# More products of constants at the front, and copies of probabilities ahead of exponentials in the fourth and the last four units

## The chip, the cores and the metric

The kernel runs on one core of one Trainium2 chip. The metric is device time in microseconds (us) of one execution. Three runs of the kernel before took 1654.76, 1656.32 and 1657.05 us; their median, 1656.32 us, is the time before.

A core has five engines that run side by side, each through its own list of instructions in order: PE (TensorE, matrix products; PEld are its weight loads), DVE (VectorE), ACT (ScalarE), POOL (GpSimd) and SP (SyncE, which here only issues transfers). An instruction waits at the head of its engine's list until what it reads is there and what it overwrites has been read; all that stands behind it on that engine waits too. SP's list of transfers obeys the same rule: a transfer whose source isn't ready holds up the transfers behind it.

## The reference, cut to what matters

The input x has 32 sequences of 100 tokens with 512 features, the context 32 sequences of which the first 100 tokens matter under the causal mask. A cross-attention with 16 heads of 32 features is added to x, and then a feed-forward part, a shared expert for all tokens plus 16 experts that each take 12 tokens of every sequence:

```python
q = (Q @ WQ.T).reshape(B, Sq, NHEAD, D_K).transpose(0, 2, 1, 3)
k = (K @ WK.T).reshape(B, Skv, NHEAD, D_K).transpose(0, 2, 1, 3)
v = (V @ WV.T).reshape(B, Skv, NHEAD, D_K).transpose(0, 2, 1, 3)
scores = jnp.einsum('bhqd,bhkd->bhqk', q, k) / jnp.sqrt(jnp.float32(D_K))
scores = jnp.where(causal, scores, -jnp.inf)
attn = jax.nn.softmax(scores, axis=-1)
y = jnp.einsum('bhqk,bhkd->bhqd', attn, v)
...
x = x + y @ Wfc.T + bfc                      # Q is layernorm(x), K and V the context
x = x + experts(layernorm(x)) + shared(layernorm(x))
```

## The kernel before

Large products are made of two halves: each operand is split into a rounded part and the rest, `split` (L103) with a copy on ACT and a subtraction on DVE, and `mm3` (L49, its products are line L56) sums three products per piece. A group of one output tile is therefore 12 products.

**Units.** The attention works in `NU` = 32 units. Unit u is four sequences (`sb`) and one group of four heads (`c`): u = 4 sb + c. Counting from 0, the fourth unit is u = 3, the last four are u = 28 to 31. The steps of a unit are spread over three rounds of the loop (L576), a software pipeline whose order is written out by hand for PE, ACT, DVE, SP and POOL: in round u the kernel makes the queries of unit u (`qproj`, `qkeep`), the softmax of unit a = u - 1, and the values of unit back = u - 2. For one unit the steps are:

- `scores`: 16 products into a PSUM tile sc, of which there is one.
- `sm_max` (DVE, L278) and `sm_sub` (POOL, L287) for each half (hb = 0, 1: two sequences each); `sm_exp` (ACT, L293, two instructions for a half); `sm_sum` (DVE, L298 and L299) and `sm_mul` (POOL, L304) for each half.
- `p_turn(u, b)` for b = 0 to 3: four transposes of probabilities on PE (L310) into a PSUM tile ms, of which there are two, used in turn; `p_keep(u, b)`: the copy of these on ACT (L315), which empties the bank.
- `values`: 16 products (L325) into the next ms tile; `y_keep`: a split of y (L104, L105) and its store to DRAM (yD, issued by SP at L335).

Between these steps stand the projections of the context's keys and values: `kproj`/`kkeep` (a copy on ACT at L226 and a store kD<-kk that SP issues at L232), `vproj`/`vkeep` (L206, L208). `kload` (L237) and `vload` (L242, one load of 800 KB for four units) read them back. PSUM tiles kv, of which there are two, hold the projections in turn.

In a round the copies of b = 0, 1 follow `sm_exp(a, 0)`, and those of b = 2, 3 follow `sm_exp(a, 1)` and the key projection. Round u = 2 alone has all four turns and copies ahead of both exponentials.

**The front.** `prologue` (L340) begins with `WARM` = 8 products of a tile of constants by itself (L345); their result isn't used, and they need no load. Then come the loads and splits of WK, the first context block, WV and the second block, and the groups kproj(0, 0..3), vproj(0, 0..1), kproj(1, 0..3).

**The end of the attention.** Unit 28 is the last round of the loop; in it the last block's `kproj(8, 3)` stands between the turns of b = 0, 1 and of b = 2, 3, and `kkeep` behind all copies. `vload` for the last four units stands ahead of that `kkeep`, and so its transfer ahead of the transfer kD<-kk. Then `pr.load_y()` (L704) loads yh and yl (L1099), the attention's result of the first 384 tokens, and `last_units` (L431) writes out the rounds 29 to 31 together with the first steps of the feed-forward part, in `pr` (class `Prep`): `fc(i)` (12 products of yh, yl with Wfc into a kv tile), `add` (DVE, L1119, reads that tile), `bias` (POOL, L1110), `stats`, `rsqrt`, `norm` (DVE, L1140), `turn` (transposes on PE at L1050, copy at L1051, rest at L1052). After them the gate and up products of the shared expert start (tile gu), and the rest of the kernel, from about 360 us on, is the feed-forward part, which the diff doesn't touch.

Of the kernel before, what the change touches and what calls it, by code (L numbers as in the profile page):

```python
# [29 lines left out]
BUF = dict(cr=4, raw=6, cx=8, x=2, xr=3, v=2, kk=2, kt=2, vt=2, q=3, p=5, pt=5, y=2, pj=2, sc=1, tr=2)  # L30
GROUPS = [3, 2, 3, 3, 3, 3, 3, 3, 2]
GMAX = 384
WARM = 8
NSLOT = B * CAP
NST = NSLOT // 128
EPS = 1e-5
# [24 lines left out]
def attention(tc, K, F):  # L61
    nc = tc.nc
    with ExitStack() as ctx, ExitStack() as kvctx:
# [57 lines left out]
        def split_wc(w, c, r, eng=None):  # L121
            cs = slice(c * 128, (c + 1) * 128)
            split(WH[w][:, :, cs], WL[w][:, :, cs], r.rearrange("p (d n) -> p d n", d=NC4), eng)
# [122 lines left out]
        def qproj(u):  # L246
            sb, c = divmod(u, NC4)
            cs = slice(c * 128, (c + 1) * 128)
            nh, nl = cur["xh", sb], cur["xl", sb]
            pq = ps_kv.tile([128, D], F32, name="kv")  # L250
            mm3(nc, pq[:, 0:SB], [((WH[2][:, d, cs], WL[2][:, d, cs]),
                                   (nh[:, d, :], nl[:, d, :])) for d in range(NC4)])
            return pq

        def qkeep(u, pq):
            q = qp.tile([128, SB], F32, name="q")
            nc.scalar.copy(q, pq[:, 0:SB])
            cur["q", u] = q

        def scores(u):  # L260
            q, kt = cur["q", u], cur["k", u]
            sc = ps_sc.tile([S, 4, D], F32, name="sc")
            for b in range(4):
                cs = slice(b * S, (b + 1) * S)
                for h in range(4):
                    rows = slice(32 * h, 32 * h + 32)
                    nc.tensor.matmul(sc[:, h, cs], q[rows, cs], kt[rows, cs], start=True, stop=True)  # L267
            cur["sc", u] = sc
# [20 lines left out]
        def sm_exp(u, hb):  # L289
            p = cur["p", u, hb][0]  # L290
            for bb in range(2):
                b = u // NC4 * 4 + hb * 2 + bb
                nc.scalar.activation(p[:, bb], p[:, bb], AF.Exp, scale=rstd[:, b:b + 1])  # L293
# [8 lines left out]
        def sm_mul(u, hb):  # L302
            pv, sm = cur["p", u, hb][1], cur["sm", u, hb]
            nc.gpsimd.tensor_tensor(pv, pv, sm[:, :, None].to_broadcast([S, 8, S]), ALU.mult)  # L304
# [8 lines left out]
        def p_keep(u, b):  # L313
            pt = ptp.tile([128, 4, S], F32, name="pt")[0:S]
            nc.scalar.copy(pt, cur["tp", u, b][0:S, :, 0:S])  # L315
            cur["pt", u, b] = pt
# [20 lines left out]
        NU = nsb * NC4  # L337
# [78 lines left out]
        def turns(u, *bs):  # L416
            for b in bs:
                p_turn(u, b)

        def keeps(u, *bs):  # L420
            for b in bs:
                p_keep(u, b)
# [8 lines left out]
        def last_units(pr):  # L431

            gp, mt = nc.gpsimd, pr.pt

            def kt_bank():
                return ps_kv.tile([128, D], F32, name="kv").rearrange("p (c t) -> p c t", c=NC4)

            def maxes(u):
                for hb in range(2):
                    sm_max(u, hb)  # L440
                    sm_sub(u, hb)

            u = NU - 3
            kload(u)
            for i in range(pr.nt):
                pr.load_x(i)
            kload(u + 1)
            sm_max(u - 1, 0)
            sm_sub(u - 1, 0)
            y_keep(u - 3)  # L450
            sm_max(u - 1, 1)
            sm_sub(u - 1, 1)
            qkeep(u, qproj(u))
            turns(u - 2, 0, 1)
            keeps(u - 2, 0, 1)
            turns(u - 2, 2, 3)
            sm_exp(u - 1, 0)
            keeps(u - 2, 2, 3)
            sm_exp(u - 1, 1)
            for hb in range(2):  # L460
                sm_sum(u - 1, hb)
                sm_mul(u - 1, hb)
            pr.fc(0)
            F.chunk_load()
            values(u - 2)

            u = NU - 2
            scores(u - 1)
            y_keep(u - 3)
            pr.add(0)  # L470
            pr.bias(0)
            maxes(u - 1)
            pr.bias(1)
            pr.stats(0)
            pr.rsqrt(0)
            qkeep(u, qproj(u))
            turns(u - 2, 0, 1)
            keeps(u - 2, 0, 1)
            sm_exp(u - 1, 0)
            sm_exp(u - 1, 1)  # L480
            pr.fc(1)
            pr.norm(0)
            for hb in range(2):
                sm_sum(u - 1, hb)
                sm_mul(u - 1, hb)
            turns(u - 2, 2, 3)
            keeps(u - 2, 2, 3)
            pr.add(1)
            kload(u + 1)
            F.chunk_load()  # L490
            pr.store(0)
            pr.bias(2)
            values(u - 2)

            u = NU - 1
            scores(u - 1)
            y_keep(u - 3)
            maxes(u - 1)
            pr.fc(2)
            pr.add(2)  # L500
            pr.stats(1)
            pr.rsqrt(1)
            pr.stats(2)
            pr.rsqrt(2)
            F.ask(1, lambda: ps_kv.tile([128, D], F32, name="kv"))
            F.preps[1].load_x(0)
            F.preps[1].load_x(1)
            turns(u - 2, 0, 1)
            keeps(u - 2, 0, 1)
            qkeep(u, qproj(u))  # L510
            pr.pt = kt_bank
            pr.turn(0)
            pr.pt = mt
            pr.norm(1)
            pr.store(1)
            turns(u - 2, 2, 3)
            keeps(u - 2, 2, 3)
            pr.norm(2)
            pr.store(2)
            sm_exp(u - 1, 0)  # L520
            values(u - 2)
            sm_sum(u - 1, 0)
            sm_mul(u - 1, 0)
            y_keep(u - 2)
            pr.turn(1)
            sm_exp(u - 1, 1)
            sm_sum(u - 1, 1)
            sm_mul(u - 1, 1)
            F.chunk_cast(0, 0)

            scores(u)
            F.chunk_low(0, 0, gp)
            F.preps[1].fc(0)
            maxes(u)
            turns(u - 1, 0, 1)
            keeps(u - 1, 0, 1)
            turns(u - 1, 2, 3)
            keeps(u - 1, 2, 3)
            F.preps[1].fc(1)
            F.chunk_cast(0, 1)  # L540
            sm_exp(u, 0)
            sm_sum(u, 0)
            sm_mul(u, 0)
            pr.turn(2)
            sm_exp(u, 1)
            F.chunk_low(0, 1, gp)
            values(u - 1)
            sm_sum(u, 1)
            sm_mul(u, 1)
            y_keep(u - 1)  # L550
            F.chunk_cast(0, 2)
            scctx.close()
            F.open_gu()
            F.begin(pr.done())
            F.chunk_low(0, 2, gp)
            F.preps[1].add(0)
            F.preps[1].add(1)
            for i in range(3):
                F.chunk_cast(1, i)
                F.chunk_low(1, i, gp)  # L560
            F.preps[1].bias(0)
            F.preps[1].bias(1)
            turns(u, 0, 1)
            keeps(u, 0, 1)
            pr.logits()
            turns(u, 2, 3)
            keeps(u, 2, 3)
            F.begun()
            values(u)
            pr.tokens()  # L570
            y_keep(u)

        with tc.manual_schedule(engines={mybir.EngineType.Pool}):
            wq = prologue()
            ahead = False
            for u in range(NU - 3):  # L576
                sb, c = divmod(u, NC4)
                a, back = u - 1, u - 2
                a = a if a >= 0 else None
# [3 lines left out]
                kv = j in blocks  # L583
# [47 lines left out]
                if u == 1:  # L631
# [1 line left out]
                    wq_keep(2, wq[2])  # L633
                    sm_sum(a, 0)
                    sm_mul(a, 0)
                if a is not None and u > 2:
                    sm_exp(a, 0)
                if back is not None:
                    p_turn(back, 0)
                    p_turn(back, 1)  # L640
                    p_keep(back, 0)
                    p_keep(back, 1)
                if u == 2:
                    p_turn(back, 2)
                    p_turn(back, 3)
                    p_keep(back, 2)
                    p_keep(back, 3)
                    split_wc(2, 3, wq[3])
                    xt_split(1, 0)
                    sm_exp(a, 0)  # L650
                if xn:
                    x_stats(*xn)
                    if xn[1] == 3:
                        x_rstd(xn[0])
                if a is not None and u > 1:
                    sm_exp(a, 1)
                    sm_sum(a, 0)
                    sm_mul(a, 0)
                pk = kproj(j, ck) if kv else None
                if kv and vv:  # L660
                    kkeep(j, ck, pk)
                if u == 1:
# [2 lines left out]
                    sm_mul(a, 1)  # L665
                if c == 1 and u > 1 or u == NU - 4:
                    vload(sb)
                if back is not None and u > 2:
                    p_turn(back, 2)
                    p_turn(back, 3)  # L670
                    p_keep(back, 2)
                    p_keep(back, 3)
                if u == 1:
                    vkeep(j, ck, vproj(j, ck))
                    wq_less(3, wq[3])
                if kv and not vv:
                    kkeep(j, ck, pk)
                if a is not None and u > 1:
                    sm_sum(a, 1)
# [733 lines left out]
```

## Time and profile before

| what | value |
|---|---|
| median of three runs | 1656.32 us (1654.76 to 1657.05) |
| the profiled execution | 1656.77 us, its span 1655.0 us |
| PE busy, 0 to 15 us | 13.41 of 15.00 us |
| PE busy, 15 to 60 us | 44.23 of 45.00 us |
| PE busy, 60 to 75 us | 13.11 of 15.00 us |
| PE busy, 75 to 310 us | 234.25 of 235.00 us |
| PE busy, 310 to 360 us | 46.00 of 50.00 us |
| PE busy, 360 to 1655 us | 1291.29 of 1295.00 us |
| share of the chain that ended last | PE 95%, DVE 1%, POOL 1%, DMA 1%, ACT 1% |

The times are of one profiled execution; the span goes from its first to its last instruction, and the 1.77 us between span and time lie around it. Busy time of PE is modelled from the starts of pipelined products, so a busy PE can still be slow: where products of one shape follow each other, the distance of their starts tells the pace. The rows of the timeline show start, duration, engine, line, operation, the tiles written and read, the shape and a count; brackets tell how long the engine was idle before and what ended that.

The fourth unit's round lies at about 56 to 68 us, the rounds 28 to 31 at about 303 to 350 us.

### The profile page before, as it was taken

What the parts mean: (1) busy time and instruction counts of PE and PEld (TensorE: products, weight loads), DVE (VectorE), ACT (ScalarE), POOL (GpSimd) and SP (SyncE); (2) the same over time, 40 slices, a digit from 0 to 9 for tenths busy, and PEclk for the clock granted to TensorE, in tenths of its full rate; (3) what the DMA queues carried; (4) which work ended last, traced back from release to release, by engine and by line L of the source; (5) the groups of instructions that cost most, each with busy time, mean ns of one, the idle gap of its engine ahead of it and who ended that gap; (6) DMA issues with size and microseconds to landing.
All of it is one profiled execution on the core that took longest, in us unless ns stands there. A gap on an engine that the chain in (4) does not pass through costs nothing.

```text
span 1655.0 us, 27948 instructions
## 1 busy us (share of the span) xinstructions
PE 1642.3 (99%) x10722; PEld 1506.0 (91%) x10722; DVE 913.1 (55%) x2178; ACT 697.4 (42%) x1152; POOL 623.9 (38%) x501
## 2 busy tenths in 40 slices
PE   9999999999999999999999999999999999999999
PEld 8888888889899998999999999999999999999998
DVE  6878777665433434344655555555555555555542
ACT  4666666553111211123444444444444444444442
POOL 2778777660111011010743334433344443344001
PEclk9999999999999999999999999999999999999999
DMA  8566665645231223211545555455555455555452
GB/s 258 169 198 200 202 195 173 211 153 185 90 108 49 88 88 111 81 62 30 191 161 159 150 164 170 144 162 150 159 169 161 148 152 161 162 163 160 138 160 62
DMA packets 113493, 243.81 MB, mean 147 GB/s; under 512 B 16609, under 2 KB 64834, under 8 KB 113360
## 3 DMA queue, kind: packets, MB, share of 16 engines
q1 hardware_dynamic: 99856, 216.34, 39.8%
q0 software_dynamic: 13088, 25.22, 8.0%
q8 instruction: 84, 1.38, 0.3%
q14 instruction: 49, 0.40, 0.1%
q10 hardware_dynamic: 416, 0.48, 0.1%
HBM read 188.25 MB, written 53.73 MB: 146 GB/s over the span
## 4 chain that ended last, share of the span: by engine, by line
PE 95%; DVE 1%; POOL 1%; DMA 1%; ACT 1%; issue 1%; SPq 0%; POOLq 0%; ACTq 0%
PE gu L56 49%; PE dn L56 25%; PE kv L56 11%; PE m L56 3%; PE ms L310 2%; PE ms L325 1%; PE sc L267 1%; POOL p L287 1%; DMA yD<-y 0%; DVE p L278 0%; DMA yh<-yD 0%; PE m L1194 0%; DMA raw<-wA 0%; ACT pt L315 0%; POOL p L304 0%
## 5 line engine op out<-in xcount | busy, mean ns | idle before, releaser
L56 PE MATMUL gu<-xh,whl 128*128 128x384 f32 (+1 forms) x3200 | 641.2, 332 | 0.0
L56 PEld LDWEIGHTS gu<-xh,whl 128*128 128x128 f32 x3200 | 555.8, 188 | 20.3 <-issue 1.2
L1018 POOL DMA_INDIRECT gx<-xnD,iq x192 | 245.2, 1277 | 395.6 <-DVE big L1061 296.3
L56 PE MATMUL dn<-whl,hh 128*128 128x512 f32 x1168 | 366.3, 395 | 0.0
L821 DVE TENSOR_TENSOR whl<-wraw,whl 128x1536 fp32r<-128x1536 f32 x142 | 249.7, 1759 | 197.8 <-ACT whl L820 178.6
L56 PE MATMUL gu<-xl,whl 128*128 128x384 f32 (+1 forms) x1600 | 335.9, 331 | 0.0
L56 PEld LDWEIGHTS gu<-xl,whl 128*128 128x128 f32 x1600 | 279.1, 188 | 0.2 <-DVE xl L1052 0.2
L855 ACT CAST hh<-g 128x384 fp32r<-128x384 f32 (+1 forms) x200 | 101.0, 505 | 409.8 <-DVE g L852 379.2
L56 PEld LDWEIGHTS dn<-whl,hh 128*128 128x128 f32 x1168 | 215.7, 188 | 35.7
L852 DVE TENSOR_TENSOR g<-g,gu 128x384 f32<-128x384 f32 (+1 forms) x200 | 108.3, 541 | 251.0 <-PE gu L56 245.1
L820 ACT CAST whl<-wraw 128x1536 fp32r<-128x1536 f32 x142 | 209.8, 1477 | 57.2 <-PE dn L56 53.4
L56 PE MATMUL dn<-whl,hl 128*128 128x512 f32 x584 | 230.5, 395 | 0.0
L851 ACT ACTIVATE g<-gu 128x384 f32<-128x384 f32 (+1 forms) x200 | 96.2, 481 | 229.4 <-PE gu L56 229.4
L856 DVE TENSOR_TENSOR hl<-g,hh 128x384 fp32r<-128x384 f32 (+1 forms) x200 | 111.8, 559 | 114.3 <-ACT hh L855 113.8
L1073 POOL DMA_INDIRECT out_dram<-x,isl x48 | 77.7, 1619 | 171.0 <-ACT x L1072 161.2
L56 PEld LDWEIGHTS dn<-whl,hl 128*128 128x128 f32 x584 | 109.5, 188 | 26.1
L287 POOL TENSOR_TENSOR p<-p,mx 100x800 f32<-100x800 f32 x64 | 103.7, 1636 | 35.9 <-DVE mx L278 33.3
L304 POOL TENSOR_TENSOR p<-p,sm 100x800 f32<-100x800 f32 x64 | 97.4, 1528 | 35.6 <-DVE sm L299 26.2
L278 DVE CUSTOM_DVE_ANT_0 p<-sc,mask 100x100 f32<-100x100 f32 x512 | 95.5, 255 | 0.5 <-PE sc L267 0.5
L1110 POOL TENSOR_TENSOR x<-x,bfc 128x512 f32<-128x512 f32 x23 | 30.4, 1345 | 155.6 <-DMA x<-x 154.0
L293 ACT ACTIVATE p<-p,rstd 100x400 f32<-100x400 f32 x128 | 73.6, 624 | 17.6 <-POOL p L287 16.9
L1062 ACT CAST xh<-big 128x512 fp32r<-128x512 f32 x59 | 36.6, 621 | 101.4 <-DVE big L1061 101.4
(158 smaller groups left out, 1581.2 us busy)
## 6 DMA issues: line engine op xcount, KB each, us to landing
wraw<-wE SPq DMA_DIRECT2D x144, 768.0 KB
yD<-y SPq DMA_DIRECT2D x31, 400.0 KB
xr<-xT SPq DMA_DIRECT2D x32, 200.0 KB
vD<-vt SPq DMA_DIRECT2D x25, 256.0 KB
v<-vD SPq DMA_DIRECT2D x8, 800.0 KB
xnD<-xn SPq DMA_DIRECT2D x25, 256.0 KB
out_dram<-x SPq DMA_DIRECT2D x25, 256.0 KB
kt<-kD SPq DMA_DIRECT2D x31, 200.0 KB
```

The lines of the kernel that those rows point to most:

```text
L56: r = nc.tensor.matmul(out, t[0][a], t[1][b], start=(first and i == 0), stop=(last and i == n - 1))
L278: nc.vector.tensor_tensor_reduce(out=p[:, bb, h, :], in0=sc[:, h, cs], in1=mask, scale=ISCALE, scalar=NEG, op0=ALU.add, op1=ALU.max, accum ...
L287: nc.gpsimd.tensor_tensor(pv, pv, mx[:, :, None].to_broadcast([S, 8, S]), ALU.subtract)
L304: nc.gpsimd.tensor_tensor(pv, pv, sm[:, :, None].to_broadcast([S, 8, S]), ALU.mult)
L820: nc.scalar.copy(h, r)
L821: nc.vector.tensor_tensor(l, r, f32(h), ALU.subtract)
L851: nc.scalar.activation(g[:, 0:t], pg[:, 0:t], AF.Gelu)
L852: nc.vector.tensor_tensor(g[:, 0:t], g[:, 0:t], pu[:, 0:t], ALU.mult)
L855: nc.scalar.copy(hh[:, 0:t], g[:, 0:t])
L856: nc.vector.tensor_tensor(hl[:, 0:t], g[:, 0:t], f32(hh[:, 0:t]), ALU.subtract)
L1018: nc.gpsimd.indirect_dma_start(out=g[:, k, :], out_offset=None, in_=self.K.xn.rearrange("t (a f) -> (t a) f", f=128), in_offset=bass.Indir ...
L1073: ins = nc.gpsimd.indirect_dma_start(out=self.K.out, out_offset=bass.IndirectOffsetOnAxis(ap=r.isl[:, i:i + 1], axis=0), in_=o, in_offset= ...
```

## The change

It has four parts.

- `WARM` is 11 instead of 8.
- Round u = 3 gets the order of u = 2: turns and copies of b = 2, 3 directly after those of b = 0, 1, then `sm_exp(a, 0)`, `sm_exp(a, 1)`, and then the key projection.
- Round u = 28: `kproj`, the turns and copies of b = 2, 3 and `kkeep` come ahead of `sm_exp(a, 1)`. On PE the order stays; on ACT the copies and the copy kk pass two exponentials; on SP the transfer kD<-kk now stands ahead of the transfer v<-vD of `vload`.
- `last_units`: in round 29 `fc(0)` comes between the two pairs of turns, followed on ACT by `sm_exp(u - 1, 0)`, the copies of b = 2, 3 and `sm_exp(u - 1, 1)`; in round 30 the turns and copies of b = 2, 3 come between the exponentials' halves, behind `fc(1)`; in round 31 the turns and copies of b = 2, 3 come ahead of `pr.turn(0)`, and `scores(u)` and the second half of the softmax ahead of `pr.turn(1)`.

No instruction is added but the three products of constants, and none is taken away.

```diff
-WARM = 8
+WARM = 11
...
             turns(u - 2, 0, 1)
             keeps(u - 2, 0, 1)
+            pr.fc(0)
+            sm_exp(u - 1, 0)
             turns(u - 2, 2, 3)
-            sm_exp(u - 1, 0)
             keeps(u - 2, 2, 3)
             sm_exp(u - 1, 1)
...
-            pr.fc(0)
             F.chunk_load()
...
             sm_exp(u - 1, 0)
+            pr.fc(1)
+            turns(u - 2, 2, 3)
+            keeps(u - 2, 2, 3)
             sm_exp(u - 1, 1)
-            pr.fc(1)
             pr.norm(0)
...
-            turns(u - 2, 2, 3)
-            keeps(u - 2, 2, 3)
             pr.add(1)
...
             qkeep(u, qproj(u))
+            turns(u - 2, 2, 3)
+            keeps(u - 2, 2, 3)
             pr.pt = kt_bank
             pr.turn(0)
             pr.pt = mt
             pr.norm(1)
             pr.store(1)
-            turns(u - 2, 2, 3)
-            keeps(u - 2, 2, 3)
...
             y_keep(u - 2)
-            pr.turn(1)
+            scores(u)
             sm_exp(u - 1, 1)
             sm_sum(u - 1, 1)
             sm_mul(u - 1, 1)
+            pr.turn(1)
             F.chunk_cast(0, 0)
 
-            scores(u)
...
-                if a is not None and u > 2:
+                if a is not None and u > 3:
                     sm_exp(a, 0)
...
-                if u == 2:
+                early = u in (2, 3)
+                if early:
                     p_turn(back, 2)
                     p_turn(back, 3)
                     p_keep(back, 2)
                     p_keep(back, 3)
+                if u == 2:
                     split_wc(2, 3, wq[3])
                     xt_split(1, 0)
+                if early:
                     sm_exp(a, 0)
...
+                pk = None
+                if u == NU - 4:
+                    pk = kproj(j, ck)
+                    p_turn(back, 2)
+                    p_turn(back, 3)
+                    p_keep(back, 2)
+                    p_keep(back, 3)
+                    kkeep(j, ck, pk)
                 if a is not None and u > 1:
                     sm_exp(a, 1)
                     sm_sum(a, 0)
                     sm_mul(a, 0)
-                pk = kproj(j, ck) if kv else None
+                if kv and not pk:
+                    pk = kproj(j, ck)
...
-                if back is not None and u > 2:
+                if back is not None and not early and u < NU - 4:
                     p_turn(back, 2)
...
-                if kv and not vv:
+                if kv and not vv and u < NU - 4:
                     kkeep(j, ck, pk)
```

## The prediction

> **What bounds the kernel now.** I read the page first, then the PE timeline of the three places that the change touches, then what ACT and SP do there, then the DMA rates by stretch.
>
> ```profile
> span 1655.0 us, 27948 instructions
> PE 1642.3 (99%) x10722; PEld 1506.0 (91%) x10722; DVE 913.1 (55%) x2178; ACT 697.4 (42%) x1152; POOL 623.9 (38%) x501
> PEclk9999999999999999999999999999999999999999
> ```
>
> PE is the chain: only a pause of PE, or products that run slowly, can give time back. The timeline (start, length, engine, line, operation) shows both at the front:
>
> ```profile
> 1.08 3.78 PE L345 MATMUL ms<-avg 128*128 128x128 f32 x16 [1.08 <-DVE avg L342]
> 4.90 0.58 PE L56 MATMUL kv<-cxh,wh 128*128 128x256 f32 x1
> 5.66 0.58 PE L56 MATMUL kv<-cxl,wh 128*128 128x256 f32 x1 [0.17 <-DVE cxl L139]
> ...
> 9.39 0.58 PE L56 MATMUL kv<-cxh,wl 128*128 128x256 f32 x1
> ...
> 13.61 0.41 PE L56 MATMUL kv<-cxh,wh 128*128 128x256 f32 x1
> 13.83 0.41 PE L56 MATMUL kv<-cxl,wh 128*128 128x256 f32 x1
> ...
> 14.55 0.28 PE L56 MATMUL kv<-cxh,wh 128*128 128x256 f32 x1
> 14.67 0.28 PE L56 MATMUL kv<-cxl,wh 128*128 128x256 f32 x1
> ```
>
> Read the distances of starts, not lengths: equal products stand 0.213 us apart up to 14.04 and 0.118 us after (the page's PEclk line is flat and does not show it). The slow pace ends after an unbroken run of 4.65 us (9.39 to 14.04); the constants' run of 3.78 us did not end it, and pauses follow it.
>
> In the fourth unit (u = 3) PE pauses for the copies of probabilities (L315), which stand behind an exponential on ACT:
>
> ```profile
> 63.23 0.86 PE L310 MATMUL ms<-ident,p 100*100 100x100 f32 x8 [1.83 <-POOL rstd L161]
> 61.56 1.15 ACT L293 ACTIVATE p<-p,rstd 100x400 f32<-100x400 f32 x2 [2.46 <-POOL p L287]
> 62.61 0.86 ACT L315 COPY pt<-ms 100x400 f32<-100x400 f32 x2
> ```
>
> The releaser that the row names is not it: the turns need the bank of tile ms that the first L315 copy empties. In the last units:
>
> ```profile
> 314.75 0.86 PE L310 MATMUL ms<-ident,p 100*100 100x100 f32 x8 [0.39 <-ACT pt L315]
> 316.43 1.19 PE L56 MATMUL kv<-wfh,yh 128*128 128x512 f32 x4 [0.81 <-DMA yh<-yD]
> 328.82 0.89 PE L325 MATMUL ms<-pt,v 100*32 100x100 f32 x32 [0.80 <-ACT pt L315]
> 304.55 0.31 SPq L242 DMA_DIRECT2D v<-vD  x1
> 311.14 0.32 SPq L232 DMA_DIRECT2D kD<-kk  x1
> 311.52 0.43 SPq L1099 DMA_DIRECT2D yh<-yD  x1
> 306.00:311.00 5.00, 5.00 (x88) 4.53 (x90) 2.87 (x13) 4.49 (x10) 3.80 (x3) 1.00 0.55 164
> 316.00:327.00 11.00, 10.57 (x108) 8.66 (x109) 7.25 (x40) 4.79 (x11) 7.44 (x6) 1.00 1.05 382
> ```
>
> Two waits are for L315 copies, one for the load of yh. The last two rows end in DMA share and GB/s.
>
> **The front.** Three more products cost 3 x 3.78 / 8 = 1.42 us: PE reaches the first real product at 1.08 + 11 x 0.4725 = 6.28 instead of 4.90. Nothing is lost by it: twelve products at 0.213 end at 8.84, the next group starts at 8.67 now, and its third product waits for wl until 9.39 in either case (without that cover they would cost up to 1.4). What is gained is that PE runs unbroken from 1.08 (by 6.28 all but the last slice of cxl is split, and that one, ready at 7.36, is used at about 8.2). A run longer than 3.78 and at most 4.65 us ends the slow pace: between 4.9 and 5.7, at any rate before 9.39. Then kproj(0,1), its third product at 9.39, ends at 9.39 + 10 x 0.118 = 10.57, kproj(0,2) and (0,3) take 12 x 0.118 = 1.41 each, to 13.39, where vproj(0,0) starts at 15.63 now. Two vproj of 12 x 0.2275 = 2.73 reach 18.85. Here it catches: kproj(1,0) needs the bank that the vt copy empties, ACT does that behind two xnh casts, and these wait for xr ("0.28 <-DMA xr<-xT", 17.71); vt ends at 19.30. The xr issues are paced by SP (one every 0.5 us from 9.37 to 14) and the DMA share there is 0.97 to 1.03, so they do not come sooner. kproj(1,0) starts at 19.35 instead of 21.10: **-1.75 us**, bounds -2.2 (as far as vproj) and +0.2 (pace not changed). Later data has slack: values(0) has more than 4 us after the load of v.
>
> **The fourth unit.** All four turns stand together, the copies ahead of the exponential, as in u = 2, where the second pair waited 0.54 us (48.19 to 48.73). PE goes on with 0.54 instead of 2.00 us of pause: -1.46. But the next unit's scores need DVE and POOL: exp(2,0) still waits for POOL until 61.5, exp(2,1) moves only from 63.37 to 63.08 (POOL ends 63.04), so sum(2,1) comes 0.8 earlier, two L105 rows of 2.39 in all follow, then the maxes, POOL's subtraction and the copies: turns(2,2,3), at 73.83, come at 73.08. **-0.75**, bounds -1.46 and 0.
>
> **The last four units.** In u = 28 the diff places kkeep ahead of exp(27,1), and so ahead of vload, which it also passes on SP. SP takes its issues in turn. kk now follows the copies 2, 3: kproj ends at 308.67, the first copy 0.60 later (as 344.40 to 345.00), kk 0.76 behind (309.86 to 310.62): 310.03, and kD<-kk is issued 0.52 after that, at 310.55. v<-vD, issued at 304.55 before, now waits behind it until 310.93; yh and yl come at 311.3 and 311.8 with 800 KB ahead of them. v took all of 306 to 311 (164 GB/s x 5 us = 820 KB) and some of 312; the landing events of the trace put its eight loads 7.1 to 9.4 us behind their issue, and what is issued after v lands after v. I take 7.6: v at 318.5. yh is 786 KB, at 382 GB/s 2.06 us more: 320.6 instead of 316.4.
>
> In u = 29 fc(0), which needs yh, now stands ahead of turns(27,2,3), which filled part of that wait. fc(0) 320.65 to 323.9 (3.24 as now), turns 0.64, copy 0.60 + 0.45 behind their start, values(27) 325.0 instead of 319.67: +5.3. exp(28,1) stands behind those copies, so DVE and POOL follow: sum(28,1) ends 327.75, maxes(29) 331.65, POOL's product 329.3, bias 330.6, two subtractions of 1.52 333.6. u = 30 gives some back (its 0.80 wait shrinks): values(28) at 333.7, +4.9. u = 31: POOL's bias(1) 1.3 and rsqrt 0.9 to 335.8, norm 0.55, sum 1.2, product 1.5: turns(29,0) 339.1 instead of 333.44, +5.65. Behind it pr.turn(0) waits for add(2) and pr.turn(1) for norm(1), as now; the removed waits of 0.38 and 0.54 return there. Gate-up, 350.79 now, starts at about 356.5: **+5.7**. Lower bound: v, kD and yh share 382 GB/s evenly, (0.82 + 0.20 + 0.79) MB / 0.382 = 4.7 us from 311.3, yh at 316.0; the same walk then ends at +0.9, since turns have left the wait. Upper: v takes 8.4, +6.5.
>
> **A long pause.** PE then rests from 314.2 to 320.6. The nearest rows are 1.83 us (63.23), after which the pace is full, and the front, where a cold PE needed 4.65 us: a price between 0 and 4.65 x (1 - 0.118 / 0.213) = 2.1. 6.4 is far from both; I take half, **+1.0**. [...]
>
> **Sum.** -1.75 - 0.75 + 5.7 + 1.0 = +4.2. The profiled execution took 1656.77 (span 1655.0, 1.77 around it), which makes 1660.97; the runs' median lies 0.45 lower, so I put all times on the median 1656.32: **1660.5**, own range 1658.5 to 1662.7.
>
> **Rivals.**
> - *yh is not late* (0.18): the 800 KB overlap it, end part +1.2, no long pause: -1.75 - 0.75 + 1.2 = -1.3, 1655.0. For it: share 0.55 in 306 to 311 leaves DMA room. Against: issues behind other v loads landed behind them. [...]
> - *The removed waits stay removed* (0.14): faster. Softmax keeps up and yh lands as now; PE saves 1.75 + 1.46 + the waits of 312 to 360 on pt, xn and x, 1.5 + 0.4 + 0.5 + 0.2 = 2.6: -5.8, 1650.5. It decides if exp(28,1), behind the copies, ends before 318 as it does now (317.86). Against: fc(0) alone ends at 319.67.
> - *The front's pace does not change* (0.15): the run from 1.08 doesn't count. -0.75 + 5.7 + 1.0 = +5.95, 1662.3. For it: 3.78 us did not do it.
> - The forecast has 0.53.
>
> **Numbers.** 0.2% is 3.3 us (about what a measurement of this kernel tells from no change): 1653.0 and 1659.6. Faster: 0.14. Same: 0.18 and a quarter of the forecast's 0.53, 0.31. Slower: 0.55. The range 1654.2 to 1664.0 leaves out the faster case and tails.
>
> **What would show it.** Products 0.118 apart before 9.39; kproj(1,0) near 19.4; the second pair of turns of u = 3 about 0.5 us behind the first, then a pause near 1 us in u = 4; v issued behind kD<-kk; a wait of some 6 us on yh ahead of fc(0), 0.2 us apart or more afterwards if the pace falls. An fc(0) starting before 317 makes the prediction wrong.

## The result, and the profile after

The changed kernel took 1664.61 us (median of 6 runs, 1663.14 to 1667.26), the kernel before 1656.68 beside it (6 runs): a ratio of 1.0048, with a 95% interval of 1.0038 to 1.0059. It is slower by 7.9 us, where 4.2 were forecast; 1664.61 lies 0.6 us beyond the end of the range. The profiled execution took 1663.14 us. From its page, the span, the engines' busy time and the clock by slices:

```profile
span 1661.4 us, 27962 instructions
PE 1642.9 (99%) x10728; PEld 1505.8 (91%) x10728; DVE 915.1 (55%) x2178; ACT 697.9 (42%) x1152; POOL 625.3 (38%) x501
PEclk9999999999999999999999999999999999999999
```

Busy times hardly moved and the clock's line is as flat as before, with slices of 41 us. What was lost can only be seen close up. Compare the starts of the same PE instructions in both traces: from kproj(1,0) at 18.73 us on the changed kernel is 2.4 us ahead, at the third turn of u = 4 it is 1.4 us ahead, at 313 us 2.0 us ahead, and from 360 us to the end 6.4 us behind. So 8.4 us are lost in the last four units.

The front, timeline of PE in the changed kernel (start, length, engine, line, operation, shape, count, idle time before and its releaser):

```profile
1.08 5.07 PE L345 MATMUL ms<-avg 128*128 128x128 f32 x22 [1.08 <-DVE avg L342]
5.80 0.56 PE L56 MATMUL kv<-cxh,wh 128*128 128x256 f32 x1
6.16 0.41 PE L56 MATMUL kv<-cxl,wh 128*128 128x256 f32 x1
6.37 0.32 PE L56 MATMUL kv<-cxh,wl 128*128 128x256 f32 x1
6.53 0.28 PE L56 MATMUL kv<-cxh,wh 128*128 128x256 f32 x1
...
8.75 0.39 PE L56 MATMUL kv<-cxh,wl 128*128 128x256 f32 x1 [0.23 <-DVE wl L105]
...
18.73 0.74 PE L56 MATMUL kv<-cxh,wh 128*128 128x256 f32 x4
```

The last row is the start of kproj(1,0); in the profile before it is this one:

```profile
21.10 0.64 PE L56 MATMUL kv<-cxh,wh 128*128 128x256 f32 x4
```

The pace opens at about 6.4 us. That is later than the 4.9 to 5.7 us that the prediction named first, but before the third product of the second group (8.75), as it had it. The fourth unit, timelines of PE, DVE and POOL:

```profile
57.36 0.87 PE L310 MATMUL ms<-ident,p 100*100 100x100 f32 x8 [0.34 <-ACT pt L315]
67.15 0.44 PE L56 MATMUL kv<-xnl,wh 128*128 128x400 f32 x1 [0.83 <-DVE xnl L105]
72.41 0.86 PE L310 MATMUL ms<-ident,p 100*100 100x100 f32 x8 [1.27 <-ACT pt L315]
63.78 3.31 DVE L105 TENSOR_TENSOR xnl<-xr,xnh 128x400 fp32r<-128x400 f32 x2
65.67 2.31 POOL L139 TENSOR_TENSOR cxl<-cr,cxh 128x384 fp32r<-128x384 f32 x2
```

The pause of 2.0 us ahead of the second pair of turns is gone, 0.5 is left of it; two others have taken its place (by distances of starts 1.0 and 1.4 us). The last units, timelines of PE and of SP's issues:

```profile
312.98 0.55 PE L310 MATMUL ms<-ident,p 100*100 100x100 f32 x4 [0.89 <-DVE y L105]
318.73 2.04 PE L56 MATMUL kv<-wfh,yh 128*128 128x512 f32 x4 [5.20 <-DMA yh<-yD]
320.57 1.91 PE L56 MATMUL kv<-wfl,yh 128*128 128x512 f32 x4
322.28 1.84 PE L56 MATMUL kv<-wfh,yl 128*128 128x512 f32 x4
323.95 0.85 PE L310 MATMUL ms<-ident,p 100*100 100x100 f32 x8
325.10 0.89 PE L325 MATMUL ms<-pt,v 100*32 100x100 f32 x32 [0.29 <-ACT pt L315]
308.68 0.32 SPq L232 DMA_DIRECT2D kD<-kk  x1
309.09 0.32 SPq L242 DMA_DIRECT2D v<-vD  x1
309.46 0.49 SPq L1111 DMA_DIRECT2D yh<-yD  x1
```

v is issued 0.41 us behind the store of kk and, by the landing events of the trace, lands at 316.65, 7.6 us later; yh lands at 318.59, 1.94 behind v. fc(0) waits 5.2 us for it and then takes 5.22 us instead of 3.24: the products of one term stood 0.23 apart before and stand 0.43 apart here. The table of stretches (the columns that matter are the first, the length and PE's busy time behind it, and the last three: granted clock, DMA share, GB/s) names the reason:

```profile
313.66:317.07 3.41, 0.00 (x0) 0.00 (x0) 1.90 (x10) 1.60 (x3) 2.26 (x3) 1.00 1.06 276
317.07:320.48 3.41, 1.75 (x4) 1.49 (x5) 0.00 (x0) 0.00 (x0) 1.33 (x1) 0.50 1.06 372
320.48:323.90 3.42, 3.42 (x9) 2.51 (x8) 0.00 (x0) 0.00 (x0) 0.00 (x0) 0.50 1.06 400
323.90:327.30 3.40, 3.11 (x76) 2.60 (x75) 0.71 (x1) 2.31 (x5) 0.00 (x0) 1.00 0.42 163
```

After 3.41 us without a product the clock is at half for 6.83 us.

### The profile page after: what moved, and what is told of

It reads as the page before. It is cut to its first block, busy times and chain, and to the rows that moved or that the text cites. A ratio compares the mean times of both kernels' runs of the same rounds, so it can differ in the third digit from the quotient of the medians.

```text
span 1661.4 us, 27962 instructions
## 1 busy us (share of the span) xinstructions
PE 1642.9 (99%) x10728; PEld 1505.8 (91%) x10728; DVE 915.1 (55%) x2178; ACT 697.9 (42%) x1152; POOL 625.3 (38%) x501
## 4 chain that ended last, share of the span: by engine, by line
PE 93%; DVE 2%; POOL 2%; issue 1%; ACT 1%; DMA 1%; SPq 0%; POOLq 0%; DVEq 0%; ACTq 0%
PE gu L56 49%; PE dn L56 25%; PE kv L56 10%; PE m L56 3%; PE ms L310 2%; PE ms L325 1%; PE sc L267 1%; POOL p L287 1%; DMA yh<-yD 1%; DVE xnl L105 0%; POOL p L304 0%; DVE sm L298 0%; PE m L1206 0%; ACT p L293 0%; DVE p L278 0%
## 5 line engine op out<-in xcount | busy, mean ns | idle before, releaser
L298 DVE TENSOR_REDUCE sm<-p 100x8 f32<-100x800 f32 x64 | 62.8, 982 | 34.1 <-ACT p L293 32.8
```

## The experiments

All were timed in five rounds; the kernel before took 1657.41, 1657.28 and 1656.59 us beside the three groups (22 to 29 runs each).

**One part of the change at a time.** The front alone:

```diff
-WARM = 8
+WARM = 11
```

> The kernel before with eleven products of constants at the front and nothing else changed. If the front is worth what the changed kernel's trace shows (the same products 2.1 us earlier from 14 us on) and no later wait takes it back: products 0.118 us apart from about 6.5 us, kproj(1,0) near 18.8 us, 1654.6 us, ratio 0.9987. If a later wait with a fixed time of its own absorbs it (the pause of 0.73 us at 181 us, the load of yh at 316 us), the products run early at 20 us but the end is where it was: 1656 to 1657 us. The prediction's own term was -1.75 us.

Measured: 1656.56 us, 0.9997 (0.9985 to 1.0008). By the ratio the front is worth 0.5 us and may be worth nothing; the -1.75 of the prediction lies inside the interval (-2.5 to +1.3 us), off its middle, so the timing alone does not exclude it. The traces say why it should be less. The clock's opening came at 14.13 us in the profile before. But in three other kernels whose front is that of the kernel before (this group's next two, and the one with the last two rounds alone) it came at 10.62, 4.91 and 5.57, and kproj(1,0) started at 19.42, 19.10 and 20.63, against 21.10 in the profile before; in the last of the three the clock fell again, from 8.98 to 12.40. In these traces the changes of the clock lie whole steps of 3.41 us apart (more on this below). In the profile before, PE was busy for 3.20 us of the step that ends at 7.30 and for 3.12 of the one that ends at 10.71, and the pace stayed low after both (products 0.213 us apart up to 14.04); it opened after the first step that was busy throughout (3.41 us, to 14.13). So the same front opened at one step or another. With eleven constants it came between 4.61 and 6.80 in ten traces, and kproj(1,0) started at 18.6 to 21.4, in the middle at 19.4. In seven of these traces it waited 0.27 to 2.38 us for the copy vt, which stands on ACT behind casts that wait for the load of xr, as here in the timelines of PE and ACT of the kernel with v first and both old orders:

```profile
21.05 0.74 PE L56 MATMUL kv<-cxh,wh 128*128 128x256 f32 x4 [1.84 <-ACT vt L206]
19.99 0.52 ACT L104 CAST xnh<-xr 128x400 fp32r<-128x400 f32 x1 [1.71 <-DMA xr<-xT]
```

So the profile before showed one late opening among several, and xr's landing, which the prediction took as fixed, moves by as much as was to be gained (the cast shown begins at 19.99; in the trace before it and the one ahead of it begin at 17.71 and take 1.10 together).

The fourth unit alone (on the kernel before):

```diff
...
-                if u == 2:
+                early = u in (2, 3)
+                if early:
                     p_turn(back, 2)
...
+                if early:
                     sm_exp(a, 0)
...
```

> The kernel before with the order of the fourth unit (u = 3) alone changed. The prediction's step: the pause of 2.0 us at 63.2 shrinks to about 0.5, 0.75 us of it come back in the unit behind, so the products from 74 us on stand 0.75 us earlier, 1655.9 us. The rival, read from the changed kernel's trace: the pause shrinks as said, but the exponential that now stands behind four copies delays the casts of xn and the next softmax, so that pauses of about 1.0 us in qproj(4) and 1.4 us ahead of the third turn of u = 4 take its place and the products stand 0 to 0.7 us later than before, 1656.7 to 1657.3 us.

Measured: 1657.20 us, 1.0002 (0.9992 to 1.0011). A gain of 0.75 (0.99955) isn't excluded by the ratio; the trace has to tell. The softmax of this unit begins 1.47 us ahead of the trace before (POOL's subtraction at 58.53 against 60.00); the third turn of u = 4 is only 0.84 us ahead (72.99 against 73.83), so 0.63 us are lost on the way, with the same two pauses as in the changed kernel (0.90 and 1.44). The rows of the kernel before, to be held against those of the changed kernel above (63.78 and 65.67):

```profile
66.13 2.39 DVE L105 TENSOR_TENSOR xnl<-xr,xnh 128x400 fp32r<-128x400 f32 x2
66.36 1.73 POOL L304 TENSOR_TENSOR p<-p,sm 100x800 f32<-100x800 f32 x1 [0.49 <-DVE sm L299]
68.06 1.34 POOL L139 TENSOR_TENSOR cxl<-cr,cxh 128x384 fp32r<-128x384 f32 x1
```

The second half's sum comes only 0.29 us earlier (63.23 against 64.99, less the lead), and the two subtractions behind it take 3.32 instead of 2.39, which makes +0.64. The length lies in the second one. In the trace before it takes 1.90 us and ends 0.44 behind the end of POOL's product; in this one it misses that gap, stands through POOL's first cxl as well and takes 2.87. In the trace before, one that begins while POOL rests (79.71) takes 0.57, and one that begins beside POOL's subtraction (71.84) takes 0.72 and ends 0.43 behind a row of POOL. So in these rows a subtraction of DVE that begins beside a row of POOL ends 0.43 or 0.44 us behind the end of a row of POOL. It is no chance of one execution: the second subtraction takes 2.86 or 2.87 us in all eight traces with the new order of this unit and 1.89 or 1.90 in all six with the old one. No run moves cxl alone, so the cause is read from rows and not tested.

What was left of the lead did not last in this trace. yh was issued 0.71 us earlier than in the trace before (310.81 against 311.52) and landed 0.24 later (316.62 against 316.38), with v first as before; fc(0) waited 1.76 us for it instead of 0.81 and then ran at half the clock. Stretches of this trace (first the length and PE's busy time, then the clock, DMA share and GB/s as the last three columns):

```profile
314.40:317.81 3.41, 1.65 (x11) 1.28 (x10) 1.74 (x3) 2.76 (x6) 2.17 (x2) 1.00 1.07 390
317.81:321.22 3.41, 3.41 (x13) 2.16 (x15) 0.64 (x2) 0.00 (x0) 2.07 (x2) 0.50 1.07 389
```

The last four units alone (eight constants, the old order of the fourth unit; the rest as changed):

```diff
-WARM = 11
+WARM = 8
...
-                early = u in (2, 3)
+                early = u == 2
```

> The changed kernel with eight products of constants and the old order of the fourth unit: only the last four units are changed. The prediction has +5.7 us for the late yh and +1.0 for the long pause, 1663.4 us. The rival, from the changed kernel's trace, in which fc(0) takes 5.2 us instead of 3.24: the pace falls for the whole of fc(0) and beyond, +2.0 instead of +1.0, and the chain behind it adds a little more, +8.4 in all, 1665.1 us. If the slow fc(0) depends on when within a fixed time of the clock the pause falls, then fc(0) here, which starts some 2 us later than in the changed kernel, may run at another pace: 3.24 us long, and 1662 to 1663 us.

Measured: 1665.33 us, 1.0049 (1.0034 to 1.0064): the last units carry all of the loss, +8.1 us (5.6 to 10.6). In its trace fc(0) waits 5.8 us; the clock is at half from 318.93 to 325.76, and its first eight products (from 322.20 on) run in that time.

**What in the last units.** v issued first:

```diff
                 if u == NU - 4:
+                    vload(sb)
                     pk = kproj(j, ck)
...
-                if c == 1 and u > 1 or u == NU - 4:
+                if c == 1 and u > 1:
```

> The changed kernel with one line moved: in u = 28 the load of v is issued ahead of kproj and kkeep, so that it does not stand behind the store of kk on SP. If the late v (and yh behind it) is what costs, v is issued before 305 us, yh lands near 315 instead of 318.6, fc(0) takes 3.24 us again with no slow products, and the time falls by 5 to 7 us to 1657.5 to 1659.5 us. If the order on PE (fc(0) ahead of the turns of u = 27, with the exponential of u = 28 behind their copies) is what costs, the time stays within 2 us of the changed kernel, 1662.5 us or more.

Measured: 1658.21 us, 1.0016 (1.0006 to 1.0025), 6.4 us below the changed kernel by the medians and 5.3 by the ratios. Its timelines of SP and PE:

```profile
303.85 0.31 SPq L242 DMA_DIRECT2D v<-vD  x1
309.88 0.32 SPq L232 DMA_DIRECT2D kD<-kk  x1
310.25 0.43 SPq L1112 DMA_DIRECT2D yh<-yD  x1
315.20 1.16 PE L56 MATMUL kv<-wfh,yh 128*128 128x512 f32 x4 [0.47 <-DMA yh<-yD]
316.20 1.09 PE L56 MATMUL kv<-wfl,yh 128*128 128x512 f32 x4
```

One line on SP is two thirds (by the ratios) to four fifths (by the medians) of the loss: v is issued 6 us ahead of kk's store, yh lands at 315.06, and the granted clock is 1.00 from 311 to 317.5.

With v first and fc(0) of u = 29 back behind the turns and the exponentials:

```diff
-            pr.fc(0)
-            sm_exp(u - 1, 0)
             turns(u - 2, 2, 3)
+            sm_exp(u - 1, 0)
             keeps(u - 2, 2, 3)
...
+            pr.fc(0)
             F.chunk_load()
```

> The changed kernel with v issued ahead of kproj in u = 28 and the old order of u = 29, that is both suspects undone; the front, u = 3, the early copies of u = 28 and the orders of u = 30 and 31 stay. If the two together are all of the loss, 1656.5 to 1657.5 us, 1 us below the kernel with v alone put first (1658.2). If the orders of u = 30 and 31 cost the rest, 1658 us or more.

Measured: 1655.48 us, 0.9992 (0.9983 to 1.0001); once more, beside the third group:

> The kernel with v put first and the old order of u = 29, the front and the new order of the fourth unit kept, once more beside the others: 1655.5 us as in its first five rounds, within 0.8, and at or below the kernel before; if that was luck, as the kernel before within 0.5.

1656.01 us, 0.9998 (0.9989 to 1.0007). fc(0)'s place on PE was the rest, 2.2 to 2.7 us by the medians (3.0 to 4.0 by the ratios). The first of the two is 1 us below the expected range. The kernel isn't faster than the kernel before by more than these runs can tell. The same order with v still late:

> The changed kernel with the old order of u = 29: fc(0) behind turns(27,2,3) and both exponentials, as before; v is still issued behind the store of kk, so yh is as late. If fc(0)'s place on PE matters once yh is late, the turns, copies and exponentials run while PE waits for yh, values(27) starts 0.6 to 1.3 us sooner and the softmax of u = 28 some 4 us sooner: 1661.5 to 1663.5 us. If the late yh alone sets the end, 1664 us or more.

Measured: 1663.13 us, 1.0032 (1.0020 to 1.0044), 1.5 below the changed kernel, in the expected range; the two intervals overlap. Its trace, PE:

```profile
317.22 0.55 PE L310 MATMUL ms<-ident,p 100*100 100x100 f32 x4 [0.29 <-ACT pt L315]
321.69 2.08 PE L56 MATMUL kv<-wfh,yh 128*128 128x512 f32 x4 [3.92 <-DMA yh<-yD]
323.57 1.91 PE L56 MATMUL kv<-wfl,yh 128*128 128x512 f32 x4
```

The turns fill the wait, as they did before the change, but 3.9 us of it are left, and fc(0) behind them takes 5.42 us (321.69 to 327.11) instead of 3.24. The orders of u = 30 and 31 alone, on the kernel before:

```diff
             sm_exp(u - 1, 0)
+            pr.fc(1)
+            turns(u - 2, 2, 3)
+            keeps(u - 2, 2, 3)
             sm_exp(u - 1, 1)
-            pr.fc(1)
...
-            pr.turn(1)
+            scores(u)
             sm_exp(u - 1, 1)
```

> The kernel before with the orders of u = 30 and 31 alone changed. By the prediction the waits of 0.38 and 0.54 us return elsewhere and the copies ahead of the exponentials give nothing: 1657.4 us, as before, within 0.7. If these orders cost the 2.6 us that were left when v went first and no product ran slowly, 1659 us or more; if they shorten waits as they say, 1656 us.

Measured: 1656.43 us, 0.9996 (0.9987 to 1.0005): no difference that the ratio can tell, and no cost. In its trace the five pauses of PE between 328 and 346 us in the trace before (by distances of starts 0.96, 0.37, 0.54, 0.78 and 0.75) have become four (0.46, 1.02, 0.34 and 0.72), 0.86 us less; the median is 0.85 lower. So these orders may bring what they say as long as nothing ahead of them is late.

**What the low clock costs.** Constants into fc(0)'s own bank while yh is on its way, 40 at first:

```diff
+            zp, pm = pr.pm(), pr.pm
+            for _ in range(40):
+                nc.tensor.matmul(zp[:, 0:128], avg, avg, start=True, stop=True)
+            pr.pm = lambda: zp
             pr.fc(0)
+            pr.pm = pm
```

> The changed kernel with 40 products of constants into fc(0)'s own bank just ahead of fc(0), which keep TensorE busy while yh is on its way; fc(0) writes over them. yh comes no sooner. If the pause of 5.2 us lowers the clock, the low stretch behind it is gone, fc(0) takes 3.24 us instead of 5.2, and the time falls by 2 to 3.4 us (one to two stretches of 3.41 us at half the clock are worth 1.7 us each) to 1661.2 to 1662.6 us. If the pace costs what the prediction put (1.0) or the slow products lie behind something else, it falls by 1 us or less, 1663.6 us or more.

Measured: 1666.66 us, 1.0056 (1.0043 to 1.0070), 2 us slower than the changed kernel by the medians (the intervals overlap), which neither theory expected. All its five runs have a mean clock of 1.000, but the dose was wrong; PE in its trace:

```profile
315.72 9.12 PE L458 MATMUL kv<-avg 128*128 128x128 f32 x80
324.59 1.18 PE L56 MATMUL kv<-wfh,yh 128*128 128x512 f32 x4
```

Each constant is two passes of 0.111 us, so forty fill 8.87 us, and yh, which landed at 321.67, waited 2.9 us for them. With twenty:

> The changed kernel with 20 products of constants ahead of fc(0) instead of 40. Forty took 8.87 us (two passes of 0.111 us each), so fc(0) stood ready behind yh for about 2.9 us; twenty take 4.44 us and end before yh lands. If the low clock is worth its two stretches, no stretch at half the clock is left near 320 us, fc(0) takes about 2.9 to 3.2 us instead of 5.2, and the time is 2 to 3 us below the changed kernel's 1664.6: 1661.6 to 1662.6 us. If the clock costs the predicted 1.0 or less, 1663.6 us or more.

Measured: 1663.50 us, 1.0043 (1.0030 to 1.0055), 1.1 below the changed kernel, though the intervals overlap; it lies between the two expectations. The trace is of the fastest of its five runs (1661.52 us). PE in it:

```profile
312.93 4.65 PE L458 MATMUL kv<-avg 128*128 128x128 f32 x40
318.01 1.20 PE L56 MATMUL kv<-wfh,yh 128*128 128x512 f32 x4 [0.42 <-DMA yh<-yD]
319.04 1.10 PE L56 MATMUL kv<-wfl,yh 128*128 128x512 f32 x4
321.33 1.20 PE L56 MATMUL kv<-wfh,yl 128*128 128x512 f32 x4 [1.18 <-DMA yl<-yD]
```

The clock stays full, the first eight products stand at the old pace, and then fc(0) waits for yl. From its start to the next turns it takes 4.36 us, 0.86 less than in the changed kernel: about one of the two microseconds lies over the wait for yl. yl landed 3.3 us behind yh here and 2.1 in the thirteen other traces; why is open. So these runs tell only roughly what the low clock cost in the changed kernel.

**A stretch at half the clock in the fourth unit.** In the trace with the front alone the products behind the pause of 2.0 us ran at half the clock, in the profile before they did not. Stretches of the first, then of the second:

```profile
60.20:63.62 3.42, 1.57 (x13) 1.24 (x12) 2.25 (x8) 2.96 (x7) 3.34 (x5) 1.00 0.11 38
63.62:67.03 3.41, 3.41 (x10) 2.66 (x9) 2.91 (x4) 2.83 (x8) 2.91 (x2) 0.50 0.19 65
```

```profile
58.50:61.91 3.41, 2.89 (x21) 2.57 (x19) 3.41 (x33) 0.84 (x2) 2.27 (x3) 1.00 0.87 290
61.91:65.33 3.42, 2.10 (x14) 1.89 (x15) 1.78 (x5) 3.42 (x9) 3.34 (x4) 1.00 0.00 0
```

The changes of the clock in one trace lie whole multiples of 3.413 us apart (in the changed kernel 6.46 to 317.07 is 91 of them, and 317.07 to 323.90 two). The pause is the same 2.0 us in both traces. In the first it lies in one stretch of this grid, which is left with 1.57 us busy, in the second across two (2.89 and 2.10); that this decided is read from these rows alone. What such a stretch costs can be read from the six traces with the old order of this unit: from POOL's subtraction to the third turn of u = 4 it is 13.8 us in the three without it (one of them with the pause filled, as below) and 15.3 in the three with it, against 14.5 in all eight traces with the new order. So the new order loses 0.6 us against the old one at full clock, and gains 0.8 where the old one would have had the stretch. Two kernels test it, both with v first and the old order of u = 29: the old order of the fourth unit again, and the same with 8 constants in the pause.

```diff
+                zv = None
+                if u == 3:
+                    zv = ps_kv.tile([128, D], F32, name="kv")
+                    for _ in range(8):
+                        nc.tensor.matmul(zv[:, 0:128], avg, avg, start=True, stop=True)
                 if back is not None and not early and u < NU - 4:
                     p_turn(back, 2)
...
```

> The kernel with v put first and the old order of u = 29, with the old order of the fourth unit as well. By the traces the new order costs 0.64 us on the clock's full pace, but its shorter pause spares the stretch at half the clock that follows the pause of 2.0 us in some runs. If the first weighs more, the median is 0.3 to 0.7 us lower than the same kernel's with the new order; if the second, 0.3 to 1.0 us higher, and fewer of its runs show a mean clock of 1.000.

Measured: 1656.07 us, 0.9996 (0.9988 to 1.0005), beside 1656.01 of the same kernel with the new order: no difference.

> The kernel with v put first and the old orders of u = 29 and of the fourth unit, with 8 products of constants (1.78 us) in the bank of vproj's product while PE waits for the third turn of u = 3. If the pause of 2.0 us is what brings the stretch at half the clock in some runs, no run falls below a mean clock of 1.000 for it, and the median is 0.5 to 1.2 us below the same kernel without these products. If the pause is harmless, there is no difference within 0.4 us.

Measured: 1655.15 us, 0.9994 (0.9986 to 1.0003), 0.9 below; the intervals overlap. The counts of runs with a mean clock below 1.000 are clearer (the slow start does not count in it; the profile before shows 1.000): with the pause (the kernel before and three others) 73 of 115, with the new order of the fourth unit (three kernels without a late yh, one of them timed twice) 12 of 46, with the pause filled 1 of 11; the kernel that differs from that one by the constants alone has 6 of 12. But a low mean clock does not say where the stretch lies. Of the profiled executions that show one without a late yh, two have it behind this pause (the front alone and the last two rounds alone), the fourth unit alone has it at the wait for yh (317.82), the kernel with v first and both old orders at 21.76, behind the wait for xr, and the kernel with v first and the old order of u = 29 only in its last 1.8 us. So the counts tell of this pause among other things. In the three groups of runs, those of the kernel before have a median span of 1653.6, 1654.8 and 1653.4 us at 1.000, and of 1655.8, 1655.6 and 1655.5 at 0.999. The timeline of the filled pause:

```profile
59.73 1.95 PE L685 MATMUL kv<-avg 128*128 128x128 f32 x16
61.73 0.86 PE L310 MATMUL ms<-ident,p 100*100 100x100 f32 x8
```

So the new order of the fourth unit does bring something that the prediction had not seen, by the counts a stretch at half the clock fewer in many runs; by the traces it costs 0.6 us at full clock. That the two cancel fits the two equal medians (1656.07 and 1656.01); no run separates them.

## Why the prediction was right and where it was wrong

- **The chain that makes it slower** is as predicted, step by step: kk behind the copies, v behind kk's store on SP (predicted 7.6 us to land, measured 7.6), yh 2.06 behind v (1.94), fc(0) ahead of the turns, a wait of 6 us (5.2). In the clock of the trace before, fc(0) starts at 318.73 + 2.0 = 320.7, predicted 320.65. That v's place on SP is the cause is shown by moving that one line (-6.4 us by the medians, -5.3 by the ratios), fc(0)'s place by moving it back (another 2.2 to 2.7, or 3.0 to 4.0).
- **The front, -1.75: mis-sized.** Alone it gave -0.5 (-2.5 to +1.3), and the profile pair shows 2.4. The step that failed is taking 14.13 us as where the pace opens in the kernel before: three traces of the same front have 4.9 to 10.6. It also took the landing of xr as fixed.
- **The fourth unit, -0.75: mis-sized, with the wrong sign in the trace (+0.63 at full clock).** "sum(2,1) comes 0.8 earlier" was 0.29, the 0.29 by which the prediction itself had the exponential come sooner, as the sum follows the end of the exponential by 0.47 us in both traces; "two L105 rows of 2.39 in all" took 3.3. Alone it gave +0.3 us (-1.3 to +1.8).
- **The last four units, +5.7 and +1.0 for the pace: mis-sized.** Measured alone +8.1, in the trace +8.4. values(27) should have been 5.3 + 1.0 late and is 7.4 (325.10 against 319.67, and the lead of 2.0), because fc(0) takes 2.0 us more and not 1.0; values(28) is 7.4 late as well, so u = 30, which "gives some back" (0.4), gave nothing back: its wait is 0.76 where it was 0.80; turns(29,0) is 8.2 late where 6.65 were predicted. On the pace, fc(0) is 2.0 us longer where +1.0 was booked, the author's estimate from two rows; with the clock kept full 0.86 of the 2.0 came back in the trace.
- **The sum.** The three misses, +1.3, +1.0 and +1.4, make the 3.7 us between +4.2 and +7.9. The intervals of the first two terms are as wide as their misses, so these are told by the traces; only the sum (+6.3 to +9.8) and the last term (+5.6 to +10.6) are clear of no change by the runs. Between the two profiled executions the change is +6.4: there the front and the fourth unit gave 2.0 instead of 2.5, and the last four cost 8.4 instead of 6.7, the largest miss.
- **The rivals.** yh was late, and in all fourteen traces it landed behind v, by 1.9 to 4.3 us; the removed waits did not stay removed behind a late yh (six pauses by distances of starts, 4.1 us in all, between 334 and 353 us, where the trace before has five of 3.4); and "the front's pace does not change" named the right place for the wrong reason: it does change, but the kernel before has already had much of that in other executions.

## What to carry to other kernels

Before moving a copy that a store waits for, list what is queued behind that store: here a load of 800 KB stood behind it on SP and another load behind that, and PE waited for the last. A term read from one execution at the front, or behind a pause near 2 us, is here one draw out of several: profile more than one execution before booking it as a gain. A wait that other work fills should keep its filler; fc(0) ahead of the turns made the longer wait a bare one.

## What was not expected of the hardware

- The granted clock changes on a grid of 3.413 us that runs through the whole execution (in the changed kernel the changes at 6.46, 317.07 and 323.90 lie 91 and 2 steps apart) and begins at another point in each (the opening at 14.13 in the trace before lies 2.25 steps from that 6.46). A stretch of the grid at full clock with 0.00 us of PE's time busy (the changed kernel, from 313.66 and, at its end, from 1658.51), with 1.41 and 1.57 (the pause of the fourth unit in the last four units alone, from 59.52, and in the front alone, from 60.20) and with 1.65 (the wait for yh in the fourth unit alone, from 314.40) was followed by one at half the clock; with 2.02 (v first and both old orders, from 62.73) and 2.10 (the kernel before, from 61.91) it was not. One case does not fit: the front of the kernel with the last two rounds alone, where 2.11 us (5.57 to 8.98) were followed by a stretch at half. Busy time is modelled, so these figures are rough. A pause of 2.0 us was enough in the front alone, where it lay in one stretch.
- Twice 3.41 us at half the clock followed one wait of 5.2 us; PE was busy for only 1.75 us of the first. At the low pace, the stretches with 1.75 us busy (the changed kernel, from 317.07), 3.12 and 3.20 (the kernel before, from 7.30 and 3.89) were followed by another one like them, and those with 3.41 and 3.42 (the kernel before, from 10.71, and the changed kernel, from 320.48) by full clock.
